# Nine matmuls that nothing reads: five in fp32 behind the last key scores, four of zeros ahead of the branch, in a two-layer graph network

## The chip, the core and the metric

The kernel runs on one core of a Trainium2 chip. The metric is device time in microseconds (us) of one execution. Engines are named as the profile names them: PE (TensorE, matmuls), DVE (VectorE), ACT (ScalarE), POOL (GpSimd) and SP (issues DMAs). A line L264 is line 264 of the kernel before.

## What is computed

A graph of N = 1250 nodes with D = 512 features and E = 20000 edges, sorted by destination, goes through two layers. The part that matters here is the first layer: a graph convolution (mean over the incoming edges, then a weight) plus random-feature attention for 256 tokens, 8 heads of 64 features, 256 random features.

```python
h = relu(layernorm(x))
xn = batchnorm(h);  agg = segment_sum(xn[src], dst) / max(deg, 1)
conv = relu(agg @ W_conv + b_conv)
q, k, v = heads(dense(h), Wq), heads(dense(h), Wk), heads(dense(h), Wv)
phi(t): u = t*scale @ proj.T;  exp(u - 0.5*sum((t*scale)**2) - max(u)) / sqrt(256) + 1e-6
attn = phi(q) @ (phi(k).T @ v) / (phi(q) @ sum(phi(k)))       # the keys' max is over a whole head
x = x + batchnorm(conv + attn @ Wo + h)
# second layer: x + relu(bn(relu(bn(((1+eps)*h + A@h) @ W1 + b1)) @ W2 + b2)), A the edge counts
```

## The kernel before

**First stage (L1455 to L1618).** The edges are read, and it is tested on the chip that they are sorted and not too many for any slot. Ones and one-hot matrices on PE give, for every group of ten nodes, the place where its edges begin (`cnt`), and then the sources and destinations of its slots (`keys`, forty matmuls of 128x125 f16, L1579). Meanwhile ACT and DVE normalize the first 256 rows of x. DVE turns the keys into `js`, `prow` and `kcol` (L1616 to L1618). A helper `keep_up(n)` (L1521) issues n matmuls of zeros, 128x128 by 128x512 f16, into a PSUM tile `idle` that nothing reads; it is called with 7 at the start (L1525) and with 4 ahead of the keys' matmuls (L1570). Then every engine loads the flag `bad` (L1619) and branches (L1620): to `sorted_graph`, which is the case here, or to a general kernel.

**Building the adjacency.** `onehots` (L195) makes the one-hot rows `op` and `ok` of a batch of 50 nodes on DVE, two buffers of each; `count` (L210) multiplies them into a PSUM tile `acc` (ten matmuls of 128x100 f16, L214, two buffers), and ACT copies it to `adj` (L217). There are 25 batches.

**Beside it, the attention's first part.** `beside` (L289) is a generator that issues one piece between two batches: the transposes of the nodes' rows (L223), the key features (`features`, L233: four fp32 matmuls of 128x256 for each of four blocks, L242), and then for n = 0 to 7 the pairs (t, b), that is two halves of the tokens by four blocks of two heads (L327). For each pair:

- `scores` (L260) multiplies 64x128 by 64x256 in fp32 for both heads into the two banks of one PSUM tile `sc`, columns 0 to 255 of each; columns 256 to 511 are unused. The pool has one buffer.
- ACT copies the scores to `kf` (L330), and DVE then takes their maxima into `kmx` (L331). The next pair's scores can start only then.
- a matmul for the values (L334), and either a node or two pieces of statistics on DVE.

Behind the pairs come the maximum over all keys (`km1`, L344, its transpose L349 and `km8`, L351), the query features (L345, the same matmuls L242), the exponentials of the keys (L373), and `normed` (L278), which writes the scaled rows `xn` for the first two node blocks on DVE (L286).

**Order.** The instructions are handed to a scheduler that decides their order on each engine; an instruction passed to `order` keeps its place among the others so passed. So an added instruction can move others. Waits are on semaphores that count finished instructions of an engine. [...]

**Behind it.** The first 1250x512 product with `W_conv` (L419) with the query side of the attention (L449 to L491), the convolution's sums (L575), batchnorm, the second layer's sums (L707) and its two dense products (L764), and the output.

## Time and profile before

| | |
|---|---|
| median of 3 runs | 373.88 us (373.84 to 373.96) |
| the profiled execution, its own time | 373.36 us |
| its span, first to last instruction | 371.6 us |
| PE busy, matmuls | 357.8 us, 96% of the span |
| DVE busy | 236.0 us, 64% |
| ACT busy | 156.6 us, 42% |
| POOL busy | 34.0 us, 9% |
| mean granted PE clock | 0.993 |
| DMA | 18.06 MB, mean 49 GB/s |

How to read it: the profile is of one execution, and its span leaves out 1.8 us of that execution's time. A matmul in fp32 appears as two rows, of which each streams all columns. A row's length holds the time until its result is out, so rows overlap: the cost of one in a series is the distance between starts. In a timeline a row gives start, length, engine, line, operation, output<-inputs, shapes and count, and in square brackets the idle time of the engine before it with what ended it. A row with a count merges instructions that follow each other. Lines of the changed kernel below the first edit stand three lines lower, behind the second one five.

### The profile page before, as it was taken

What the parts mean: (1) busy time and instruction counts of PE and PEld (TensorE: products, weight loads), DVE (VectorE), ACT (ScalarE), POOL (GpSimd) and SP (SyncE); (2) the same over time, 40 slices, a digit from 0 to 9 for tenths busy, and PEclk for the clock granted to TensorE, in tenths of its full rate; (3) what the DMA queues carried; (4) which work ended last, traced back from release to release, by engine and by line L of the source; (5) the groups of instructions that cost most, each with busy time, mean ns of one, the idle gap of its engine ahead of it and who ended that gap; (6) DMA issues with size and microseconds to landing.
All of it is one profiled execution on the core that took longest, in us unless ns stands there. A gap on an engine that the chain in (4) does not pass through costs nothing.

```text
span 371.6 us, 4935 instructions
## 1 busy us (share of the span) xinstructions
PE 357.8 (96%) x1852; PEld 262.9 (71%) x1852; DVE 236.0 (64%) x586; ACT 156.6 (42%) x310; POOL 34.0 (9%) x49
## 2 busy tenths in 40 slices
PE   8799989999999999999999999999999999999992
PEld 5665554775656699998768888777777777777771
DVE  7999984659896235687887222182881788414673
ACT  6688459636665450111057402132652552122211
POOL 2000000000000005000000009620053000000000
PEclk9999999999999999999999999999999999999997
DMA  5953200000000571000000000150000000000124
GB/s 179 312 191 111 83 32 0 2 1 2 0 1 2 178 272 53 0 3 0 2 0 0 2 0 1 33 196 0 2 0 1 1 2 0 1 0 11 59 81 133
DMA packets 13413, 18.06 MB, mean 49 GB/s; under 512 B 1357, under 2 KB 6786, under 8 KB 13382
## 3 DMA queue, kind: packets, MB, share of 16 engines
q1 hardware_dynamic: 12670, 17.34, 14.0%
q10 hardware_dynamic: 712, 0.33, 0.3%
q8 instruction: 16, 0.26, 0.3%
q14 instruction: 15, 0.12, 0.1%
HBM read 15.11 MB, written 2.56 MB: 48 GB/s over the span
## 4 chain that ended last, share of the span: by engine, by line
PE 86%; DVE 10%; ACT 1%; issue 1%; DVEq 0%
PE mm L764 32%; PE mm L707 12%; PE mm L575 12%; PE hw L419 10%; PE mm L242 3%; PE mm L449 2%; PE mm L521 2%; DVE op L203 2%; PE mm L482 2%; PE acc L214 2%; PE sc L264 2%; PE mm L223 1%; PE mm L701 1%; DVE ok L203 1%; DVE kmx L331 1%; PE mm L472 1%
## 5 line engine op out<-in xcount | busy, mean ns | idle before, releaser
L419 PE MATMUL hw<-wconv,xn 128*128 128x512 f32 (+1 forms) x80 | 37.1, 604 | 0.3 <-ACT adj L217 0.3
L779 ACT ACTIVATE kept<-mm,vT 128x313 f32<-128x313 f32 x36 | 18.5, 520 | 42.9 <-PE mm L764 41.8
L707 PE MATMUL mm<-hi,adj 128*128 128x512 f32 (+2 forms) x100 | 32.1, 399 | 0.5 <-DVE hi L655 0.4
L707 PE MATMUL mm<-lo,adj 128*128 128x512 f32 (+2 forms) x100 | 31.7, 395 | 0.0
L131 ACT ACTIVATE r<-mv,epsc 128x1 f32<-128x1 f32 x16 | 4.7, 292 | 61.8 <-DVE mv L130 61.8
L764 PE MATMUL mm<-hid,w 128*128 128x313 f32 x96 | 25.9, 427 | 0.0
L419 PEld LDWEIGHTS hw<-wconv,xn 128*128 128x128 f32 (+1 forms) x80 | 14.1, 187 | 16.4 <-issue 14.8
L575 PE MATMUL mm<-adj,lo 128*128 128x416 f32 (+3 forms) x120 | 25.1, 355 | 0.0
L575 PE MATMUL mm<-adj,hi 128*128 128x416 f32 (+3 forms) x120 | 25.1, 355 | 0.0
L203 DVE TENSOR_TENSOR op<-iop,prow 128x1280 f16<-128x1280 f16 (+2 forms) x27 | 20.7, 766 | 6.0 <-PE acc L214 5.6
L784 DVE TENSOR_TENSOR hid<-mm,kept 128x313 f32<-128x313 f32 x24 | 10.9, 477 | 20.4 <-ACT kept L779 16.9
L764 PEld LDWEIGHTS mm<-hid,w 128*128 128x128 f32 x96 | 18.1, 190 | 6.9
L575 PEld LDWEIGHTS mm<-adj,hi 128*128 128x128 f32 x120 | 21.9, 189 | 1.1
L707 PEld LDWEIGHTS mm<-hi,adj 128*128 128x128 f32 (+2 forms) x100 | 18.4, 186 | 5.8 <-DVE hi L655 1.4
L575 PEld LDWEIGHTS mm<-adj,lo 128*128 128x128 f32 x120 | 21.8, 189 | 1.0
L698 DVE SCALAR_TENSOR_TENSOR z<-h,e,mm 128x512 f32<-128x512 f32 (+1 forms) x10 | 7.0, 746 | 23.6 <-PE mm L707 15.7
L707 PEld LDWEIGHTS mm<-lo,adj 128*128 128x128 f32 (+2 forms) x100 | 18.5, 186 | 4.6 <-DVE lo L648 0.2
L214 PEld LDWEIGHTS <-op 128*128 128x128 f16 x250 | 13.8, 97 | 7.4 <-issue 4.7
L214 PE MATMUL acc<-ok,op 128*128 128x100 f16 x250 | 16.1, 207 | 2.0 <-DVE ok L203 1.4
L702 ACT COPY zT<-mm 128x512 f32<-128x512 f32 (+1 forms) x10 | 5.3, 582 | 29.3 <-PE mm L701 29.3
L764 PE MATMUL mm<-tz,w 128*128 128x313 f32 x64 | 17.5, 426 | 0.0
L764 PE MATMUL mm<-hid,sw 128*128 128x313 f32 x64 | 17.5, 427 | 0.0
(254 smaller groups left out, 704.5 us busy)
## 6 DMA issues: line engine op xcount, KB each, us to landing
w<-in_L_gnn_W_dram SPq DMA_DIRECT2D x2, 2048.0 KB
xs<-in_x_dram SPq DMA_DIRECT2D x1, 2304.0 KB
out_dram<-xs SPq DMA_DIRECT2D x7, 256.0 KB
wk<-in_L_gnn_Wk_dram SPq DMA_DIRECT2D x1, 1024.0 KB
x<-in_x_dram SPq DMA_DIRECT2D x1, 1024.0 KB
v<-in_L_gnn_Wv_dram SPq DMA_DIRECT2D x1, 1024.0 KB
wconv<-in_L_gnn_W_conv_dram SPq DMA_DIRECT2D x1, 1024.0 KB
wk<-in_L_gnn_Wq_dram SPq DMA_DIRECT2D x1, 1024.0 KB
```

Of the source, the lines that this page charges most:

```text
L203: i = nc.vector.tensor_tensor(t[:, qs], iota.unsqueeze(1).to_broadcast(shape), keys[:, bt, qs].unsqueeze(2).to_broadcast(shape), ALU.is_equal)
L214: nc.tensor.matmul(acc[:, :, q * TG:(q + 1) * TG], op[:, q, :, i], ok[:, q, :, i].rearrange("p (j t) -> p j t", t=TG), start=(q == 0 and i ...
L242: nc.tensor.matmul(ps, wt[:, k, b * 128:(b + 1) * 128], hT[:, k, :TOK], start=(k == 0), stop=(k == KD - 1))
L264: nc.tensor.matmul(ps[:, a, :M], tT[a * 64:a * 64 + 64, b, t * 128:(t + 1) * 128], projT[a * 64:a * 64 + 64, :], start=True, stop=True)
L419: nc.tensor.matmul(ps[:n], xn[:, f, :n], wct[:, f, :], start=(f == 0), stop=(f == KD - 1))
L449: nc.tensor.matmul(ps[:, i, :], kf[:, t, hd, mb * 128:(mb + 1) * 128], va[:, t, hd, :], start=(t == 0), stop=(t == NT - 1))
L482: nc.tensor.matmul(pa[:, i, :], qfTs[n][:, i, mb, :], kv[:, mb, hd, :], start=(mb == 0), stop=(mb == 1))
L575: nc.tensor.matmul(ps, part[:k, j, fs], adj[:k, j, c], start=(part is hi and j == 0), stop=(part is lo and j == NJ - 1))
L707: nc.tensor.matmul(ps[:n], adj[:k, j, t * S:t * S + n], part[:k, j, :], start=(part is hi and j == 0), stop=(part is lo and j == NJ - 1))
L764: order(nc.tensor.matmul(banks[i], left[:, k, m * 128:(m + 1) * 128], right[:, k, i * NH:(i + 1) * NH], start=(p in (1, 2, 5) and k == 0), ...
L779: nc.scalar.activation(t[:, c, :], self.A[c], AF.Identity, bias=self.part(i, 0, c)[1], scale=1.0)
L784: order(nc.vector.tensor_tensor(self.part(i, j, c)[0], self.B[c], t[:, c, :], ALU.add))
```

## The change

`scores` gets a parameter `idle`. With it, that many matmuls follow the two score matmuls: `ident` (128x128 fp32) times `projT` (128x256 fp32), written to the unused columns 256 to 511 of the second bank of the same tile, kept in order. Pair 6 gets two, pair 7 three; the others, and the query scores, none. And the helper of the first stage is called a third time, with 4, behind the keys' matmuls, as PE's last instructions ahead of the load of the flag and the branch.

```diff
-    def scores(tT, t, b):
+    def scores(tT, t, b, idle=0):
+
 
         ps = sc.tile([128, 2, 512], F32, name="sc")
         for a in range(2):
             nc.tensor.matmul(ps[:, a, :M], tT[a * 64:a * 64 + 64, b, t * 128:(t + 1) * 128],
                              projT[a * 64:a * 64 + 64, :], start=True, stop=True)
+        for _ in range(idle):
+            order(nc.tensor.matmul(ps[:, 1, M:], ident, projT, start=True, stop=True))
         return ps[:, :, :M]
...
         for n, (t, b) in enumerate(pairs):
-            ps = scores(kT, t, b)
+            ps = scores(kT, t, b, {6: 2, 7: 3}.get(n, 0))
             o = 2 * b
             nc.scalar.copy(kf[:, t, o:o + 2, :], ps)
             nc.vector.tensor_reduce(kmx[:, t, o:o + 2], ps, AX.X, ALU.max)
...
                     order(nc.tensor.matmul(keys[kind][:, h, :], t[:, c:c + 128], pick[:, b, :NGR],
                                            start=False, stop=(h == 1 and b == RB - 1), skip_group_check=True))
 
+        keep_up(4)
+
 
         junk = raw.tile([S, D], F32, name="junk")
```

## The prediction

> **What bounds the kernel now.** The page's chain of waits comes first, since shares of busy time average over stages:

> ```profile
> PE 86%; DVE 10%; ACT 1%; issue 1%; DVEq 0%
> ```

> TensorE (PE) holds most of the chain and VectorE (DVE) a tenth. The question is which of them holds it where the change puts work. The chain in order of time, asked for 43 to 62 us (start, length, what):

> ```profile
> 46.57 0.60 DVE xn L286 x3
> 47.16 0.09 issue
> 47.26 0.68 DVE kmx L331
> 47.94 0.73 DVE op L203
> 48.67 0.59 DVE ok L203
> 49.26 0.73 DVE op L203
> 50.00 0.61 DVE kmx L331
> 50.61 0.14 issue
> 50.74 0.70 PE sc L264 x4
> 51.45 0.20 PE mm L349
> 51.65 1.73 PE mm L242 x8
> ```

> Until 50.7 us DVE sets the pace: one-hot rows (op, ok) and maxima of scores (kmx), end to end. From 50.74 PE does, but for ScalarE (ACT) from 58.64 to 61.03. So PE has room before 50.7, wherever DVE does not wait for it. The timeline shows who feeds whom:

> ```profile
> 45.30 0.70 PE L264 MATMUL sc<-projT,kT 64*128 64x256 f32 x4
> 45.94 0.70 PE L242 MATMUL mm<-hT,wk 128*128 128x256 f32 x2
> 46.05 0.59 ACT L330 COPY kf<-sc 128x512 f32<-128x512 f32 x1 [1.44 <-PE sc L264]
> ...
> 46.48 1.07 PE L214 MATMUL acc<-ok,op 128*128 128x100 f16 x20
> ...
> 47.99 0.70 PE L264 MATMUL sc<-projT,kT 64*128 64x256 f32 x4 [0.45 <-DVE kmx L331]
> ...
> 49.18 0.82 DVE L203 TENSOR_TENSOR op<-iop,prow 128x1280 f16<-128x1280 f16 x1
> ...
> 49.92 0.68 DVE L331 TENSOR_REDUCE kmx<-sc 128x2 f32<-128x512 f32 x1
> ...
> 51.18 0.60 DVE L286 TENSOR_SCALAR xn<-hT,gc 128x128 f32<-128x128 f32 x2
> ```

> The scores at 45.30 and 47.99 are those of pairs 6 and 7, which get the followers. The twenty accumulations at 46.48 are two batches, A and B (B's op is at 45.17); C has its op at 47.86, D at 49.18. D's op stands ahead of pair 7's maximum (49.92) on DVE.

> And the end of the first stage, where the zeros go:

> ```profile
> 5.58 1.04 PE L1523 MATMUL idle<-zeros 128*128 128x512 f16 x4
> ...
> 9.36 0.41 DVE L1618 SCALAR_TENSOR_TENSOR kcol<-js,keys 128x250 int16<-128x250 f32 x1
> ...
> 9.92 1.06 PE L223 MATMUL mm<-ident,x 128*128 128x128 f32 x8 [1.03 <-DVE kcol L1618]
> ```

> PE sits idle for 1.03 us before the first transposes, which wait for kcol.

> **Zeros ahead of the branch.** Four matmuls of 128x512 f16. The row at 5.58 took 1.04 us for the same four, and one alone 0.39, so they follow each other at (1.04 - 0.39)/3 = 0.22. Behind the last key matmul (end 8.88) they issue for 4 x 0.22 = 0.87 us and end about 9.76: inside the idle 1.03 us, before kcol is done (9.77). Cost 0, with 0.15 us to spare. If that cover is gone, because PE's load of the flag and its branch start only behind them, the transposes come up to 0.87 us later; PE has further gaps up to 17.33 (0.28 at 11.4, 0.30 at 12.9, 0.79 at 17.3), so at most 0.87 reaches the end. Between 0 and 0.87 I take 0. No instruction of another engine or queue moves here.

> **The fp32 followers themselves.** Each multiplies 128x128 by 128x256 in fp32, the shape of L242: 8 rows, two for each matmul, take 1.73 us on the chain, so one costs 0.433, and the last row ends 0.48 - 0.22 = 0.26 after its turn. Two cost 0.87, three 1.30. From both sides: nothing below 0; the scores' own fp32 rows, 64 partitions in, give 0.64/2 = 0.32 for a matmul, the slowest L242 stretch 1.92/4 = 0.48.

> **What the order does.** The program built from the change differs from the other, besides the nine matmuls, in four places, all near 45 to 51 us; nothing behind it changes order:
> - DVE: the last two xn (51.18 above) move ahead of pair 6's maximum.
> - PE: the last accumulation of batch B moves behind pair 7's scores and its three followers.
> - ACT: qT and sq move ahead of pair 7's copy of the scores, B's copy of adj behind it.
> - The copies of pairs 6 and 7 (kf) now wait for the last follower, not the last score, and the maximum waits for the copy.

> **The sum, step by step** (times of the profiled execution):
> 1. Pair 6's maximum, by DVE: two xn take 51.70 - 51.18 = 0.52 (the op after them starts at 51.70), so 47.26 becomes 47.78. By PE: scores start 45.30, followers issue from 45.94 to 46.81, end at 47.07; the copy starts 0.05 later and takes 0.59, so 47.72, with 0.05 for the signal 47.77. A tie: the two followers are hidden behind the moved xn. Should they be free, the xn still cost 0.52.
> 2. Pair 7's scores wait for that maximum: 47.99 + 0.52 = 48.51.
> 3. Scores issue for 0.64, three followers for 1.30: 50.45; they end at 50.71. B's last accumulation comes behind them and completes about 50.72 (one such row alone takes 0.22).
> 4. D's op writes the buffer that B's accumulations read, so it waits for the last of them. With 0.06 for the signal it starts at 50.78 instead of 49.18: **1.60 us later**. DVE would have been ready at 49.70, so it stalls 1.08, with nothing to hide it.
> 5. Pair 7's maximum stands behind that op: 50.78 + 0.74 = 51.52. Its copy is done by 50.76 + 0.59 = 51.35, so the wait for the followers adds nothing more.
> 6. The first query scores follow the maximum by 0.82 as before: 52.34 instead of 50.74. The maximum over pairs (km) and L349 behind it shift alike.

> ACT is not late: qT is due only for the query scores; kf of pair 7 and the copies for B and C (three of 0.6, from 50.76) are done by 52.5, before the next qT (53.42 + 1.60). From 52.34 the chain is the old one: PE to 58.6, ACT to 61.03 in the old order, PE again. The table load and exponentials at 54.27 follow PE's matmuls, so they shift too. The two xn that are no longer at 51.18 free DVE where it waits for PE anyhow (it idles 5.23 us before 59.73). So nothing is won back: span 371.6 + 1.60 = 373.2, time 373.36 + 1.60 = 374.96. That execution is 0.52 under the median 373.88, and the difference is what I carry over: 373.88 + 1.60 = **375.5**.

> **What the clock could give.** The only way in which unread matmuls can pay is a faster PE. The page's clock row reads 9 up to the last slice, and durations agree: fp32 rows at 0.216 us per 256 columns, f16 accumulations at 0.046 per 100 columns, the same at 40, 49 and 77 us. The one slow stretch is the start: there the zeros cost 0.43 us each (3.17 for seven at 1.19) against 0.22 at 5.58, so PE ran at half speed from 1.19 to about 5.5, a loss of half of 4.3 = 2.1 us. No such stretch comes back before the tail, so I take a gain of 0. [...]

> **Rivals.**
> - *The followers are nearly free* and only the moved xn count: +0.52, 374.4. At 0.32 each D's op would still start at 50.78 - 0.34, +1.26; only at about 0 is this reached. Against it: same shape as L242.
> - *The branch waits behind the zeros*: 1.60 + 0.87, 376.35. For it: no row shows PE's flag load, and PE's first row behind the branch is put down to issue. Against it: DVE goes from kcol to the next op in 0.07 us across the same branch.
> - *The clock, and faster than before*: in executions other than the profiled one it falls in the thin stretches 9 to 17 and 47.5 to 50.7 us, and full speed would be missing from 17.33 and from 50.74. Each fall costs 2.1 us by the start's rows. One fall prevented gives -0.5 net (373.4, no change); two give 1.60 - 4.2 = -2.6, 371.3. It decides from 2.35 us recovered. Against it: the rows above, and times that agree within 0.12 us.
> - *The change does nothing that counts*: excluded by the order, which delays D's op whatever the copies wait for.

> **Numbers.** Forecast 375.5 with 0.75 (its own range 375.0 to 376.0, from 0.32 to 0.48 us a follower and 0.15 for signals); branch behind zeros 0.08; followers free 0.09; one fall 0.04; two falls 0.04. Range 374.4 to 376.4, the ends of the two price rivals. Changes of 0.2% (0.75 us) are about what a measurement of this kernel tells from none; 374.4 and 373.4 lie inside: same 0.13, slower 0.83, faster 0.04.

> **What would show it.** Right: xn x5 before a maximum at 47.8; L214 split by three fp32 matmuls on ident; D's op waiting about 1.1 us for PE acc; query scores at 52.3 behind a PE gap of 1.3 us; transposes still at 9.9. Wrong: D's op at 49.7; transposes at 10.8; any L242 or L707 group shorter than before, which would be the clock.

## The result and the profile after

The changed kernel takes 375.64 us in the median of 9 executions (374.88 to 376.18), the kernel before, beside it on the same chip, 373.84 (373.26 to 374.19). The ratio is 1.0047, 95% interval 1.0036 to 1.0057: **slower by 1.3 to 2.1 us**, 1.80 by the medians. The profiled execution took 375.74, its span is 373.8 (before: 371.6), the mean granted clock 0.996 (before: 0.993). That is no faster clock: in both, the profile records half speed only at the very end, where PE has no work left, for the last 3.1 us here and the last 4.9 us before.

The shares of the chain of waits, in the changed kernel's page:

```profile
PE 85%; DVE 8%; DMA 2%; ACT 1%; issue 0%; SPq 0%; DVEq 0%
```

DVE has lost two points, and DMA appears: one piece of 5.91 us from 9.73, the wait for `x`, to which the last part returns. The chain in order of time where the followers stand (start, length, what):

```profile
47.03 1.28 DVE xn L289 x5
...
48.97 0.70 PE sc L265 x4
49.67 1.49 PE sc L268 x6
51.16 0.06 PE acc L214
51.22 0.02 issue
51.24 0.83 DVE op L203
```

In the kernel before this stretch belonged to DVE alone up to the query scores. Now PE stands in the middle of it: pair 7's scores, its three followers (six rows, 1.49), the last accumulation of batch B, and only then D's `op`. On the chain the maximum follows at 52.07 and the query scores at 52.82. The timeline of the same kernel shows what each waited for:

```profile
47.56 0.59 ACT L333 COPY kf<-sc 128x512 f32<-128x512 f32 x1 [2.49 <-PE sc L268]
...
49.60 1.56 PE L268 MATMUL sc<-projT,ident 128*128 128x256 f32 x6
...
51.24 0.83 DVE L203 TENSOR_TENSOR op<-iop,prow 128x1280 f16<-128x1280 f16 x1 [1.01 <-PE acc L214]
```

Pair 6's copy waits for the last follower (L268), D's `op` stands idle for 1.01 us and is released by `acc`, and the gap of PE ahead of the query scores grew from 0.78 to 1.15.

To compare runs, every start is given behind the start of pair 6's scores, which is called zero here. It falls between 45.19 and 46.21 us in the executions profiled below (47.02 in the run without the warming matmuls), and is 45.30 before and 45.76 after. That spread comes ahead of any follower. "D's op" is the start of its write, "hw" the first matmul of the product with `W_conv` (61.03 before, 63.10 after).

| | median, us | zero at | max. of pair 6 | scores of pair 7 | D's op | max. of pair 7 | query scores | hw |
|---|---|---|---|---|---|---|---|---|
| before | 373.84 | 45.30 | 1.96 | 2.69 | 3.88 | 4.62 | 5.44 | 15.73 |
| after | 375.64 | 45.76 | 2.47 | 3.21 | 5.48 | 6.23 | 7.06 | 17.34 |
| after minus before | +1.80 | | +0.51 | +0.52 | +1.60 | +1.61 | +1.62 | +1.61 |

From hw to the end of PE's last matmul it takes 304.27 us in both traces. So what is lost up to hw reaches PE's end in full, and nothing behind hw gained or lost.

### The profile page after: what moved, and what is told of

Its sections match the earlier page's. It is cut to its first block, busy times and chain, and to the rows that moved or that the text cites. A ratio compares the mean times of both kernels' runs of the same rounds, so it can differ in the third digit from the quotient of the medians.

```text
span 373.8 us, 4963 instructions
## 1 busy us (share of the span) xinstructions
PE 360.9 (97%) x1866; PEld 265.1 (71%) x1866; DVE 237.5 (64%) x586; ACT 156.9 (42%) x310; POOL 34.2 (9%) x49
## 2 busy tenths in 40 slices
DMA packets 13413, 18.06 MB, mean 48 GB/s; under 512 B 1357, under 2 KB 6786, under 8 KB 13382
## 3 DMA queue, kind: packets, MB, share of 16 engines
q1 hardware_dynamic: 12670, 17.34, 14.2%
## 4 chain that ended last, share of the span: by engine, by line
PE 85%; DVE 8%; DMA 2%; ACT 1%; issue 0%; SPq 0%; DVEq 0%
PE mm L767 31%; PE mm L710 12%; PE mm L578 12%; PE hw L422 10%; PE mm L242 3%; PE mm L452 2%; PE mm L524 2%; PE sc L265 2%; PE mm L485 2%; PE acc L214 2%; DMA x<-in_x_dram 2%; PE mm L704 1%; PE mm L223 1%; DVE op L203 1%; PE mm L475 1%; DVE kmx L334 1%
## 5 line engine op out<-in xcount | busy, mean ns | idle before, releaser
L422 PEld LDWEIGHTS hw<-wconv,xn 128*128 128x128 f32 (+1 forms) x80 | 14.1, 187 | 16.4 <-issue 14.8
L203 DVE TENSOR_TENSOR op<-iop,prow 128x1280 f16<-128x1280 f16 (+2 forms) x27 | 20.7, 767 | 6.8 <-PE acc L214 6.5
L701 DVE SCALAR_TENSOR_TENSOR z<-h,e,mm 128x512 f32<-128x512 f32 (+1 forms) x10 | 7.0, 745 | 23.6 <-PE mm L710 15.7
L214 PEld LDWEIGHTS <-op 128*128 128x128 f16 x250 | 13.8, 97 | 6.9 <-issue 4.7
L214 PE MATMUL acc<-ok,op 128*128 128x100 f16 x250 | 16.0, 207 | 1.7 <-DVE ok L203 1.7
```

The costliest lines, as they stand in the source:

```text
L203: i = nc.vector.tensor_tensor(t[:, qs], iota.unsqueeze(1).to_broadcast(shape), keys[:, bt, qs].unsqueeze(2).to_broadcast(shape), ALU.is_equal)
L214: nc.tensor.matmul(acc[:, :, q * TG:(q + 1) * TG], op[:, q, :, i], ok[:, q, :, i].rearrange("p (j t) -> p j t", t=TG), start=(q == 0 and i ...
L422: nc.tensor.matmul(ps[:n], xn[:, f, :n], wct[:, f, :], start=(f == 0), stop=(f == KD - 1))
```

## The experiments

Each kernel stands beside the kernel before on the same chip; the median of before there is given with it. Each still computes all of the two layers: what is added is read by nothing or writes the same value again, and otherwise only the order differs.

### Zeros alone

The followers are taken out; the four matmuls of zeros ahead of the branch stay.

```diff
-            ps = scores(kT, t, b, {6: 2, 7: 3}.get(n, 0))
+            ps = scores(kT, t, b, 0)
```

> Only the four zero matmuls ahead of the branch; the order of all other instructions is that of before. My theory: they fit into the 1.03 us in which PE is idle there, so 373.84 + 0 (within 0.3), the transposes start with the end of kcol. Rival: PE's branch waits behind them, or the 0.46 us by which pair 6's scores were late in the profile of after (45.76 against 45.30) come from them: 374.3 to 374.7, and the transposes 0.3 to 0.9 us behind kcol.

Measured: 373.8 us (before 374.25), ratio 0.9987 [0.9960, 1.0015]. Zero at 45.30, query scores at 5.44, hw at 15.72: the kernel before, to 0.01 us. The timeline of this run (L1526 are the zeros, L1623 is `kcol`) at the end of the first stage:

```profile
8.75 1.03 PE L1526 MATMUL idle<-zeros 128*128 128x512 f16 x4
...
10.04 1.06 PE L223 MATMUL mm<-ident,x 128*128 128x128 f32 x8 [0.26 <-DVE kcol L1623]
```

The zeros end at 9.78, `kcol` at 9.79, and the transposes start at 10.04, that is 0.25 behind `kcol` where before it was 0.15. In the changed kernel it is 0.24. So here PE took 0.26 us from the end of its last zero to the first transpose, and the zeros do delay it, by 0.10. That tenth is gone by pair 6's scores.

### Twelve zeros

```diff
-        keep_up(4)
+        keep_up(12)
```

with no followers, as in the run above.

> Twelve zero matmuls ahead of the branch, not four, no followers. 12 x 0.217 = 2.60 us, so the transposes start 1.6 us behind the end of kcol, not 0.15. My theory (PE has room up to 17.3, so that four are far from the end): of the 1.6 not more than 0.3 us reaches pair 6's scores, 373.8 to 374.2. Rival (the end of the first stage is on the chain that sets the end): +1.4 to +1.6, 375.3.

Measured: 374.34 (before 373.99), ratio 1.0003 [0.9978, 1.0027], inside what can't be told from no change.

```profile
9.18 2.75 PE L1526 MATMUL idle<-zeros 128*128 128x512 f16 x12
...
12.19 0.52 PE L223 MATMUL mm<-ident,x 128*128 128x128 f32 x3 [0.26 <-DVE op L203]
```

The zeros end at 11.93 and the transposes start at 12.19, 0.26 later again: now the branch waits behind the zeros, and the transposes stand 2.22 behind `kcol`, 2.07 more than before. From the end of `kcol` to zero it takes 36.22 us where before takes 45.30 - 9.77 = 35.53. So of the 2.07 us at most 0.7 arrives at pair 6. The expectation, not more than 0.3 of 1.6, was too low by the trace, unless part of the 0.7 has another cause: the run with followers alone takes 35.85 over the same distance with no zeros ahead of the branch. By that I estimate the slack of the stage at 2.07 - 0.7, about 1.4 us, in which even a delay of the full 0.87 would have been absorbed for the most part; this was not run.

### Followers alone

The third call of the helper is taken out, the followers stay.

```diff
-        keep_up(4)
```

> Only the five fp32 followers, no zeros; every engine's order is that of the whole change. My theory: all of the loss, 373.84 + 1.60 = 375.4, with the query scores 5.44 us behind pair 6's scores begun before and 7.04 to 7.06 us behind them now. Rival (zeros cost part of it): 0.3 to 0.5 us less than the whole change.

Measured: 375.4 (before 374.25), ratio 1.0032 [1.0011, 1.0052]. Zero at 45.81, then 2.47, 3.21, 5.49, 6.23, 7.06, 17.35: the row of the changed kernel, to 0.01:

```profile
45.81 0.70 PE L265 MATMUL sc<-projT,kT 64*128 64x256 f32 x4
...
51.30 0.82 DVE L203 TENSOR_TENSOR op<-iop,prow 128x1280 f16<-128x1280 f16 x1 [1.01 <-PE acc L214]
...
52.87 0.70 PE L265 MATMUL sc<-projT,qT 64*128 64x256 f32 x4 [1.15 <-DVE kmx L334]
```

By the trace the whole cost is the followers'. The times don't show this by themselves: the medians differ by 1.15 here, not 1.60, and nine of the 35 executions of before on this chip belong to a slower group that is explained under "Without the warming matmuls".

### Only pair 6's two followers

```diff
-            ps = scores(kT, t, b, {6: 2, 7: 3}.get(n, 0))
+            ps = scores(kT, t, b, {6: 2}.get(n, 0))
```

without the third call of the helper.

> Two followers behind pair 6's scores, none behind pair 7's; the two xn still move ahead of pair 6's maximum and the last accumulation of B behind pair 7's scores. My theory: only the first half of the chain is left, pair 6's maximum 0.52 later; B's last accumulation ends before DVE is free, so D's op doesn't wait: 373.84 + 0.52 = 374.4, query scores 5.96 us behind pair 6's scores. Rival (what counts is that D's op waits for B's last accumulation behind pair 7's scores, whatever follows them): +1.0 or more, with an idle stretch of DVE before D's op.

Measured: 374.51 (before 374.25), ratio 1.0001 [0.9977, 1.0026]; in the trace pair 6's maximum at 2.46, D's op at 4.38 with no wait, query scores at 5.95: +0.50 to +0.51 throughout, too little for the measured times to tell and plain in the trace:

```profile
49.51 0.22 PE L214 MATMUL acc<-ok,op 128*128 128x100 f16 x1
...
50.05 0.82 DVE L203 TENSOR_TENSOR op<-iop,prow 128x1280 f16<-128x1280 f16 x1
```

B's last accumulation still stands behind pair 7's scores, but it ends at 49.73, before DVE is free for D's `op` at 50.05. The other 1.1 us come with pair 7's three.

### Six followers at pair 7

```diff
-            ps = scores(kT, t, b, {6: 2, 7: 3}.get(n, 0))
+            ps = scores(kT, t, b, {6: 2, 7: 6}.get(n, 0))
```

without the third call of the helper.

> No zeros; two followers behind pair 6 and six, not three, behind pair 7, in the order of the change. My theory: D's op waits for B's last accumulation behind all six, so each of the three more adds its whole 0.433: +1.30 on the +1.60, 376.75, query scores 8.36 us behind pair 6's scores (7.06 with three), DVE idle 2.3 us before D's op. Rival (the wait has another cause and the followers run beside it): query scores at 7.1 to 7.5.

Measured: 376.41 (before 373.99), ratio 1.0075 [1.0049, 1.0101]. Its timeline:

```profile
49.03 2.86 PE L268 MATMUL sc<-projT,ident 128*128 128x256 f32 x12
51.97 0.82 DVE L203 TENSOR_TENSOR op<-iop,prow 128x1280 f16<-128x1280 f16 x1 [2.31 <-PE acc L214]
```

The wait of D's op is 2.31 where three followers make 1.01: 1.30 for three, **0.433 each**, and hw moves by 18.64 - 17.34 = 1.30 as well. So each of the three further followers at pair 7 cost its full price, as far as hw. The medians differ by 2.42 where 2.90 was expected; the interval, 1.8 to 3.8, holds both.

### The two xn put back

The changed kernel's followers, but the last two `xn` held behind the maximum over all pairs, so that DVE's order is that of the kernel before; the third call of the helper is out.

```diff
+                with tc.issue_after(last_max[0].ins) if j == 1 and f > 1 else ExitStack():
                     nc.vector.tensor_scalar(xn[:, f, :n], src, gain, shift, op0=ALU.mult, op1=ALU.add)
```

> All five followers, but the two xn are held behind the maximum over the pairs, so that DVE's order is that of before. My theory: pair 6's maximum now waits for the copy that waits for two followers, a tie with the xn by the sum, so nothing is won: +1.55 to +1.60, 375.4, and DVE idle about 0.5 us before that maximum. Rival (the moved xn are the cause of the first 0.52): +1.08, 374.9, and pair 6's maximum 1.96 us behind its scores' start as before.

Measured: 375.59 (before 374.25), ratio 1.0029 [1.0006, 1.0051]; pair 6's maximum at 2.42 where after has 2.47. In the timeline DVE now waits at that place:

```profile
47.91 0.69 DVE L336 TENSOR_REDUCE kmx<-sc 128x2 f32<-128x512 f32 x1 [0.38 <-ACT kf L335]
```

Two paths end there within 0.05 us, as the prediction had it: the two moved `xn`, and the two followers with the copy behind them. Taking the first away wins 0.05, and D's op is again held for 1.01 by `acc`.

### Without the warming matmuls that before has

This one is about the clock. The first two calls of the helper are taken out of the kernel before.

```diff
-        keep_up(7)
-        keep_up(4)
```

> Before without its eleven matmuls of zeros in the first stage, to price a slow clock. My theory: full speed comes 3 to 4 us later, the forty key matmuls take up to 0.105 us each and not 0.065, so the keys end 0.9 to 1.7 us later, of which 0.5 to 1.3 reaches the end: 374.3 to 375.1. A rival, by which unread matmuls buy nothing at any place of this kernel: 373.8, keys end as before.

Measured: 375.92 (before 373.99), ratio 1.0046 [1.0018, 1.0074]. Full speed begins at 15.3 us instead of 4.85, `kcol` ends at 11.17 instead of 9.77, which is inside the expectation, and zero is at 47.02 instead of 45.30. The time is above the expectation. The profiled execution has a second stretch at half speed, which has no counterpart there in the profiles of before and after. The stretches of this kernel (window; length, then PE busy, PEld, DVE, ACT, POOL, then the granted clock, the DMA share and GB/s):

```profile
49.43:52.84 3.41, 1.72 (x18) 1.11 (x18) 3.41 (x7) 2.26 (x5) 0.00 (x0) 1.00 0.00 1
52.84:56.26 3.42, 3.42 (x12) 2.41 (x9) 2.76 (x8) 0.00 (x0) 0.00 (x0) 0.50 0.02 5
```

The clock record says half speed from 52.84 to 56.26, 3.413 us. In the 3.41 us ahead of it PE was busy for 1.72, half of the time, in pieces: no gap there is longer than 0.79. From zero to hw this execution takes 17.37 instead of 15.73, so **this one fall cost 1.64 us**.

And the thin stretch is that of the kernel before: it lies between pair 7's scores and the query scores. The same length slid over the profile of before finds it thinnest here (same columns):

```profile
47.40:50.81 3.41, 1.56 (x20) 0.89 (x16) 3.41 (x6) 2.58 (x6) 0.00 (x0) 1.00 0.01 5
```

```profile
45.81:49.23 3.42, 2.44 (x28) 1.61 (x26) 3.42 (x9) 2.13 (x5) 0.00 (x0) 1.00 0.41 156
49.23:52.64 3.41, 2.54 (x21) 1.95 (x22) 3.41 (x10) 1.31 (x4) 0.00 (x0) 1.00 0.02 5
```

with shares of 0.71 and 0.74: the thin stretch lies in both. By the same estimate only a grid with an edge at about 47.1 to 47.8 would leave about as little in one window as the 0.50 ahead of the fall in this run: 0.5 to 0.75 of 3.41 us, 15 to 22% of the positions, if they are equally likely, which was not shown.

That can be set against the times. Of the 100 executions of before that ran beside the experiments, 78 took 372.93 to 375.09 (median 373.88, mean clock 0.994) and **22 took 375.26 to 376.66** (median 376.07, mean clock 0.989). In the mean of each group the clocks differ by 0.0052; over 372 us, at half speed, that is 3.9 us, about one fall of 3.413. Five of the 22 have a clock of 0.992, which the faster group reaches too, so the clock does not sort every single execution.

### A thinner stretch

If that estimate is right, the clock should fall in most executions of a kernel whose stretch is thinner still. Pair 7's maximum is taken three times, in the kernel before, so that PE waits longer for it:

```diff
-            nc.vector.tensor_reduce(kmx[:, t, o:o + 2], ps, AX.X, ALU.max)
+            for _ in range(3 if n == 7 else 1):
+                nc.vector.tensor_reduce(kmx[:, t, o:o + 2], ps, AX.X, ALU.max)
```

> The kernel before, with pair 7's maximum taken three times in place of once (the same result, written three times). No matmul is added or taken away. In the order as built two reductions (0.61 us each by the chain of before) and the two xn (0.26 each) now stand between pair 7's maximum and the maximum over pairs, so the first query scores start 1.74 us later: 7.18 us behind pair 6's scores in place of 5.44. PE is thinner there: one batch of ten accumulations (0.46) moves into the gap, the rest stays idle, so a stretch of 3.4 us holds about 0.33 of PE work in place of 0.46, without any single gap of 3 us. Theory A (the clock falls behind a stretch of 3.4 us that holds under about half its time in PE work): a window at half speed of about 3.4 us follows in most executions, mean clock 0.985 to 0.99, and costs 1.64 as in the run without the first warming matmuls; hw stands 19.1 us behind pair 6's scores, time 377.3. [...]

Measured: 378.8 (before 374.02), ratio 1.0143 [1.0102, 1.0184], mean clocks 0.979, 0.986, 0.988 and 0.991 in its four executions. The stretches of the profiled one, on its grid:

```profile
48.57:51.98 3.41, 1.50 (x24) 0.96 (x20) 3.41 (x7) 1.79 (x4) 0.00 (x0) 1.00 0.03 5
51.98:55.40 3.42, 2.50 (x7) 1.68 (x7) 2.81 (x8) 0.58 (x1) 0.00 (x0) 0.50 0.00 0
55.40:58.81 3.41, 3.41 (x9) 1.58 (x7) 1.22 (x2) 0.92 (x3) 0.00 (x0) 0.50 0.00 0
```

A window with 0.44 of PE work, its longest gap 1.29 us, and the clock halves at its end. The eight rows of L242 behind it take 3.62 us from 54.19 where before has 1.89. My size was short: the query scores stand at 7.49 rather than 7.18 (a one-hot write of 0.59 got between the maxima as well), and the fall lasted two windows, 6.83 us, not one; hw stands at 20.26 rather than 19.1. So the profiled execution went as theory A had it, and none of the four ran at the 0.993 of before's profile or in less than 378.03.

The clock halved behind little PE work at the end of the traces too. This is the last window at full speed in before, on its grid:

```profile
363.25:366.67 3.42, 1.49 (x11) 1.04 (x10) 2.94 (x8) 0.94 (x2) 0.00 (x0) 1.00 0.37 105
```

Its share is 0.44, its longest gap 1.36 us, and the clock halves at its end, though PE has no work left to lose by it. In all 13 profiles the last fall comes behind a window of 0.44 or less.

### The stretch filled by order instead of matmuls

If DVE holds the stretch, its order can be changed with no matmul added: in the kernel before, `xn` of the first block is held behind pair 5's maximum, `xn` of the second behind the maximum over pairs, and C's and D's one-hots behind the maxima of pairs 6 and 7.

```diff
+                with tc.issue_after(maxima[5 if j == 0 else 8].ins):
                     nc.vector.tensor_scalar(xn[:, f, :n], src, gain, shift, op0=ALU.mult, op1=ALU.add)
...
+            with tc.issue_after(maxima[{12: 6, 13: 7}[bt + 1]].ins) if bt + 1 in {12: 6, 13: 7} else ExitStack():
                 ready.append(onehots(bt + 1, (BG,) if bt else (2, 3)))
```

> No added matmul. DVE's order is changed by hand from what the study shows: the first four xn behind pair 5's maximum, the other four behind the maximum over the pairs, C's op behind pair 6's maximum and D's op behind pair 7's. My theory (DVE's order around the maxima sets the time up to the query scores): pair 6's scores at 45.6 (L242's last matmul goes ahead of them), pair 7's at 47.7, its maximum at 49.1, query scores at 49.9 instead of 50.74: 373.84 - 0.75 = 373.1. Rival (PE's own work up to there sets the time, the maxima only follow): 373.84, the gap moves elsewhere.

Measured: 374.31 (before 373.99), ratio 0.9998 [0.9979, 1.0017]. The query scores do stand at 4.32, 1.12 earlier, but hw at 15.09 only, and zero itself came 36.23 behind the end of `kcol` where before has 35.53. What was won was given back in two places: a matmul of the first query block (0.43) had moved ahead of pair 6's scores on PE, and on ACT an exponential had moved behind the fourth query block's copy. The rest of the 0.7 ahead of zero lies within what this distance varies by in runs whose order there is unchanged (35.51 to 35.85).

Both were mended, one after the other. First the matmul goes back behind pair 6's scores (and the last exponentials behind a copy of `adj`):

```diff
+                with tc.issue_after(scored[13].ins) if name == "q" and b == 0 and k == KD - 1 else ExitStack():
                     nc.tensor.matmul(ps, wt[:, k, b * 128:(b + 1) * 128], hT[:, k, :TOK],
...
+                with tc.issue_after(adj_copies[13].ins) if t * HEADS + o >= 8 else ExitStack():
                     nc.scalar.activation(kf[:, t, o, :], kf[:, t, o, :], AF.Exp, bias=kb[:, t, o:o + 1], scale=1.0)
```

> No added matmul. The order of the run with the held-back xn and one-hots, with two more instructions held: the fourth matmul of the first query block on PE goes behind pair 6's scores, where it stands in the kernel before, and the third group of exponentials on ACT goes behind the copy of batch 13. Theory: that run won 1.12 us at the query scores (4.32 in place of 5.44 behind pair 6's scores) and gave it back in two places, 0.4 to 0.7 by pair 6's scores starting later behind the keys' column row and 0.5 by ACT before the node stage. With the first place mended the query scores stand at 4.3 to 4.5 and pair 6's scores 35.5 behind the column row, as before; with the second, hw stands 14.6 to 14.8 behind pair 6's scores in place of 15.7. Time 373.0 to 373.2 against 373.9, that is -0.7 to -0.9. Rival (the work moves elsewhere again: ACT or DVE is late further on by as much): within 0.2 us of before.

Measured: 373.55 (before 374.02), ratio 0.9989 [0.9972, 1.0007]. Zero is 35.83 behind `kcol`, so most of that loss is back; hw is still at 15.09, the second half of the expectation failed, and the medians differ by 0.47 in place of 0.7 to 0.9. The hold on the exponentials had not moved the one that mattered: ACT still idled 0.57 ahead of the fourth query block's copy (`qT`). So that one was put ahead of it:

```diff
+            with tc.issue_after(exps[4].ins) if name == "q" and b == 3 else ExitStack():
                 nc.scalar.activation(tT[:, b, :], ps, AF.Copy, scale=DH ** -0.25)
...
-                exponentials(4)
+                exponentials({0: 5, 5: 3}.get(len(exps), 4))
```

> The run before it, with the third exponential ahead of the fourth query block's copy (qT) on ACT again, as in the kernel before: its ACT order is now that of before, its PE and DVE orders are those of that run. There ACT idled 0.57 us ahead of that copy and then had three exponentials between it and the copy of adj that hw waits for, where the kernel before has two. Theory: one exponential (0.39 to 0.41 us) moves into the idle time, the copy of adj starts at 59.7 in place of 60.1 and hw stands 14.7 us behind pair 6's scores in place of 15.1 (before 15.7); nothing behind changes, so the time is 0.4 below that run and 0.8 to 0.9 below before: 373.1 if before is at 374.0. Rival (hw is then held by something else, the last accumulation or the kv work behind it, and no gain is left at the end): hw at 15.0 to 15.1 and the time as in that run, 373.5.

Measured in the trace: hw at 14.70, as expected, and the span is 370.7 (before 371.6) although zero came 0.50 later in this execution. The timeline, with the copy that hw waits for:

```profile
59.89 0.56 ACT L217 CAST adj<-acc 128x500 fp32r<-128x500 f32 x1
...
60.50 1.12 PE L429 MATMUL hw<-wconv,xn 128*128 128x512 f32 x2 [0.37 <-ACT adj L217]
```

ACT's idle time ahead of `qT` is down to 0.18, and hw starts 1.03 nearer to zero than before; from hw to the end of PE's last matmul it is 304.24, so this gain is still there. Measured in time: 373.71 (before 374.16), ratio 0.9986 [0.9963, 1.0008], 0.45 by the medians where 0.8 to 0.9 was expected. The interval holds 1, so a version faster than before is shown in the trace of one execution and not in the times. Against the changed kernel, 1.0047 [1.0036, 1.0057], the order without matmuls is the better one.

## Why the prediction was right, and where it was not

- **Zeros ahead of the branch: cost 0, right; "0.15 us to spare", wrong.** I had the zeros end at 9.76 and left out the 0.26 that PE took here from its last zero to its first transpose. The transposes came 0.10 late, and the slack of the stage took it. The rival (the branch waits behind the zeros) is half real: with twelve zeros the transposes are late by the whole of it, but at most 0.7 of 2.07 reaches pair 6.
- **A follower's price, 0.433: right.** Six in place of three cost 1.30 more. "Followers nearly free" is out.
- **Pair 6, a tie at +0.52: right.** Measured +0.51, and one side of the tie taken away left 2.42 of 2.47.
- **D's op waits for B's last accumulation: right.** 1.01 of waiting against 1.08 forecast, +1.60 as forecast.
- **Nothing is won back behind it: right.** +1.62 at the query scores, +1.61 at hw.
- **From the profiled execution to the median.** The sum gives 1.60, the medians 1.80 with an interval of 1.3 to 2.1. The profiled executions differ by 2.2 in span, of which 0.46 was there already at pair 6's scores, ahead of any follower, and 0.18 came behind PE's last matmul. That 1.80 lies so near to the forecast is in part luck: with 22 slower executions in 100, nine of before without one have a chance of about a tenth. Beside 35 executions of before, nine of them in the slower group, the followers alone cost 1.15 by the medians and 0.9 by the means.
- **The clock: right for the executions compared, wrong as a statement.** I wrote that no slow stretch comes back before the tail and leaned on the rows of one execution and on three times that agreed within 0.12 us. In the experiments the clock did fall ahead of the tail, as the third rival had it: behind 3.41 us with 0.50 of PE work and behind 3.41 us with 0.44, the longest gaps in them 0.79 and 1.29 us. I priced a fall at 2.1 by the start's rows; the one of 3.413 us that was traced cost 1.64. (The start was misread a little too: the clock record has full speed from 4.85, not from about 5.5.) If the slower group's falls lie in before's thin stretch, it gives one in about a fifth of the executions. The followers close that stretch, but they cost 1.6 us in every execution. By the medians of the two groups, which were divided by the time itself, a fall costs 2.2, so 22% of it is 0.5 us in the mean, less than the price. Of the nine executions of before that the result rests on, up to 374.19, none is in the upper group, so nothing of it shows in the ratio. That the upper group's falls all lie in this stretch was not shown: the profile of before is without one, and single executions of the kernels whose thinnest stretch there is fuller (0.59 and more) had lower clocks too. Of those kernels 5 of 89 executions had a clock of 0.991 or less (0.988 with six followers, 0.989 with pair 6's alone, 0.990 with the xn put back, 0.988 and 0.991 in the last order), against 19 of 122 with the thin stretch as it was (before and the two runs with zeros alone). So the stretch seems to account for a good part of the falls, and not for all.

## What to carry to other kernels

An unread matmul is free only as long as nothing waits for its end (here D's op waited for B's last accumulation behind the followers of pair 7, and three more of them cost 0.433 us each): look for who reads the tile it writes and who stands behind it in its queue, and from the point where one of these has to wait, count every further one in full. Filling a thin stretch for the clock must be paid by the executions in which the clock falls there, so first read from the clock record how little PE work lay ahead of each fall (here 0.50 and 0.44 of 3.41 us), look for stretches as thin, and set how often falls occur, times what one costs (here 22% of 2.2 us), against what the filling costs (here 1.6). Where an engine other than PE makes the stretch thin, its order is the first thing to try, and each reordering has to be followed to the next place where engines meet.

## What the runs showed of the hardware

- Full speed lasted 361.81 us (in the six profiles without followers and without a fall ahead of the tail) or 365.23 (in the five with followers), 106 and 107 times 3.413, and began between 4.20 and 6.40 us in the profiles with the warming matmuls. Ahead of the tail the clock halved behind a window with 0.50 of PE work (at 52.84 us, without the warming matmuls, for 3.413 us) and behind one with 0.44 (at 51.98, with three maxima, for 6.83), and did not behind one with 0.55 (from 8.54, with two followers at pair 6). At the end of the executions it halved behind windows with 0.44 and less, and did not behind one with 0.59 (from 364.79, with followers alone). Once halved it stayed so behind a window with 0.73 (from 51.98, with three maxima).
- In the profiled execution of the changed kernel the chain runs through the load of `x`:

```profile
9.73 5.91 DMA x<-in_x_dram
```

  Up to 15.64 the statistics of `x` wait for this, where before had 0.44 of issue ahead of the same work at 15.19. Added matmuls touch no DMA queue here (13413 packets and 18.06 MB in both pages), and of the 0.46 by which pair 6's scores came later, 0.20 was there at the end of `kcol`; the run with followers alone had pair 6's scores as late (45.81), the one with zeros alone as early as before (45.30). What sets this spread of 45.2 to 46.2 was not tried.
